# Two graph-attention layers on one core: the memsets between the row gathers are taken out

## The chip, the core and the metric

The kernel runs on one core of a Trainium2 chip. The metric is the time of one execution in microseconds (us) on the device; lower is better. Three runs of the kernel before gave 4551.79, 4556.36 and 4559.20 us, so its median is 4556.36 us.

## The reference

The inputs are 6250 nodes with 256 features each, 200000 edges (source `src`, destination `dst`, sorted by destination) and 32 features for each edge. The nodes are normalised and cut at zero, and two graph-attention layers follow, the first with four heads of 64 features, the second with one head of 256. What one layer does is this (`x` is the node table, `n` the number of nodes):

```
te = relu(edge_attr @ We + be) * exp(x @ Wo + bo)[src][:, None]
s2, d2, ea2 = _add_self_loops(src, dst, te, n)
hx = (x @ Wg).reshape(n, h, f)
he = (ea2 @ Wge).reshape(-1, h, f)
al = leaky_relu(einsum(hx, a_s)[s2] + einsum(hx, a_d)[d2] + einsum(he, a_e), 0.2)
m  = segment_max(al, d2);  al = exp(al - m[d2])
al = al / segment_sum(al, d2)[d2]
out = segment_sum(hx[s2] * al[:, :, None], d2) + b
```

A self loop is added for every node, whose edge features are the mean over the node's incoming edges. Layer 0 ends with `relu(out + x)`; layer 1 adds its input, the input of layer 0 and the raw node features. So for every edge the row of its source node has to be fetched (`hx[s2]`), weighted with a softmax over the edges of one destination, and summed per destination.

## The kernel before, in words

The 200000 edges are cut into chunks of 128 (`P`), and 24 chunks (`C`) make a superchunk. A layer has 66 superchunks (`NS`): 64 of 24 chunks, then one of 14 and one of 13, 1563 chunks in all. One step of the main loop is one superchunk of one layer, so there are 132 steps; `k` counts them, and a step's superchunk within its layer is `s`.

**Prologue** (`prologue`, L203 and on). The node features are loaded, normalised and multiplied with the layer-0 weights; the resulting rows (features, attention terms, the exponential gate) are stored as a table `T[0]` in device memory. During this time GpSimd (POOL) also fetches the raw feature rows of step 0's edges with 24 indirect DMAs of its own (`first_rows`, L249); no other POOL instruction stands between two of these, apart from three places where normalisation statistics are worked out.

**Gather** (`gather`, L792 to L803). For each step, POOL issues one indirect DMA for each chunk: 128 rows of the layer's table (268 floats in layer 0, one of a row pair in layer 1) go to the 128 partitions of one slot of a tile `G` in SBUF (24 slots of 270 floats). There are three `G` tiles, used in turn (`self.gp[st["k"] % 3]`), so the gather of step `k` may start when step `k-3` has done its sums. After every indirect DMA of every step but step 0, POOL also writes zeros to a tile `gap` of 128x208 floats, which no other instruction reads:

```
            nc.gpsimd.indirect_dma_start(
                out=G[:, c, 0:L.TW], out_offset=None, in_=self.rows[L.l][0:n * (1 + L.l), :],
                in_offset=bass.IndirectOffsetOnAxis(ap=idx[:, c:c + 1], axis=0))
            if st["k"]:
                nc.gpsimd.memset(self.gap, 0.0)
```

Step 0's rows come from the prologue, so the loop of `gather` issues 1539 + 1563 = 3102 indirect DMAs. Each waits for the landing of the eighth indirect DMA before it (eight semaphores in turn), and a step's first one also for its `G` tile to be free.

**A step** (`edges`, L615 and on, is an order written out by hand; a tile framework sets semaphores, but moves nothing). In the iteration of step `k` the instructions are put out in this order: POOL gets the gather of step `k+1`; VectorE (DVE) takes `logits(k)` (its first instruction, L987, needs all rows of `G(k)`), then prepares step `k+1` (`spread`, `parts`), TensorE (PE) transposes the run maxima of step `k` (`ends`, L1010), PE and ScalarE (ACT) work out the edge features of step `k+1` (`rphase1`, L885 and L890; `rphase2`, L899; `adst`, L959), DVE goes on with `links` and `maxima` of step `k`, multiplies all rows of `G(k)` with their weights (`scale`, L1095), adds what is carried over from the step before (`carried`, L1080 to L1085), and PE sums the rows per destination (`sums`, L1105, for each of 24 chunks a product with a one-hot matrix `S`, which DVE writes at L930; the profile shows each product as two matmuls). Meanwhile DVE turns and reduces what belongs to step `k+1` (`edge_rows`, L973 and on) and finishes the nodes of step `k-1` (`finish`); in layer 0 their rows go through PE again (L1198, L430) and to the table `T[1]` of layer 1 with a DMA issued by SyncE (SP, L1239). ACT moves the sums from PSUM to `U` (`evict`, L1110).

So DVE, PE and ACT work on step `k` and prepare `k+1`, while POOL, which has nothing but gathers (and the memsets) in its queue in the middle of a layer, fetches the rows of step `k+1`. What ties POOL to the others is `G`: L987 waits for the last landing of a step's gather, and a gather waits for its tile.

**End of a layer** (`ending`, L709 and on). The last two steps are interleaved, POOL helps with the nodes there (L1178 to L1192), the last rows of `T[1]` are stored, and only then does the first gather of layer 1 start, since any of its rows may be wanted. At the end of layer 1 the last rows of the result are scattered (L1249).

Of the kernel before, what the change touches and what calls it, by code (L numbers as in the profile page):

```python
# [22 lines left out]
F32 = mybir.dt.float32  # L23
# [8 lines left out]
P = 128  # L32
# [47 lines left out]
class Kernel:  # L80
# [322 lines left out]
    def fixed_rows(self):  # L403
        nc, cp = self.nc, self.cp
        self.crow = cp.tile([1, D + self.L[0].H], F32, name="crow")
        self.cl = [cp.tile([36, P + 1], F32, name=f"cl{i}") for i in range(2)]
        for t in self.cl:
            nc.gpsimd.memset(t, -BIG)

        self.cnt = cp.tile([P, self.NS, 2], F32, name="cnt")  # L410
        self.mt = cp.tile([P, 4 * C + 4], F32, name="mt")
        self.gap = cp.tile([P, 208], F32, name="gap")
        self.fb = [cp.tile([P, 37 * C], F32, name=f"fb{i}") for i in range(2)]
        for t in [self.mt] + self.fb:
            nc.gpsimd.memset(t, 0.0)


        self.aq = [cp.tile([P, 4, 32], BF, name=f"aq{i}") for i in range(2)]
        for t in self.aq:
            nc.gpsimd.memset(t, 0.0)  # L420
        self.trow1 = []
        L1 = self.L[1]
        for i in range(2):
            self.trow1.append(cp.tile([P, 2 * L1.TW], F32, name=f"t1row{i}"))
            nc.gpsimd.memset(self.trow1[i][:, L1.TW + D:], 0.0)
# [366 lines left out]
    def gather(self, st):  # L792
        nc, L = self.nc, st["L"]
        st["G"] = G = self.G0 if st["k"] == 0 else self.gp[st["k"] % 3].tile([P, C, 270], F32, name="G")
        n = self.N
        idx = self.src[:, st["o"]:st["o"] + st["C"]]
        last = st["C"] - 1
        for c in (range(0) if st["k"] == 0 and self.CX > last else (last, *range(last))):
            nc.gpsimd.indirect_dma_start(  # L799
                out=G[:, c, 0:L.TW], out_offset=None, in_=self.rows[L.l][0:n * (1 + L.l), :],  # L800
                in_offset=bass.IndirectOffsetOnAxis(ap=idx[:, c:c + 1], axis=0))
            if st["k"]:
                nc.gpsimd.memset(self.gap, 0.0)  # L803

    def pair(self, k):

# [660 lines left out]
```

## Time and profile before

| What | Value |
|---|---|
| Median of three runs | 4556.36 us |
| Time of the profiled execution | 4555.93 us |
| Its span (first to last instruction) | 4554.1 us |
| POOL busy | 3915.8 us, 86% of the span |
| PE busy / DVE busy / ACT busy | 3065.9 / 2901.8 / 516.8 us |
| Indirect DMAs in `gather` (L799) | 3102 |
| Memsets of `gap` (L803) | 3102 |
| Mean granted TensorE clock | 0.743 |

The profile is one execution taken by the hardware profiler. Times are in us unless marked ns. A line of the table of groups reads: code line, engine, operation, what is written <- what is read, shape, count, then the busy time and the mean ns of one, then the time that the engine was idle just before these instructions and what ended most of that idle time; "issue" means that the engine waited for nothing that the profile shows. A line of the timeline reads: start, duration, engine, code line, operation, and in brackets the idle time before it and what ended it. For an indirect DMA on POOL the duration is the time that POOL itself works on it; when the data has landed is told apart from that ("DMA to landing"). In the table of stretches each engine has its busy time and its number of instructions, then come the granted TensorE clock as a share of full speed, the share of time that the 16 DMA engines were busy, and GB/s. The chain of work that ended last reaches back only 0.38 and 0.71 us in this profile (it ends at a wait of the program's end), so it does not help here.

### The profile page before, as it was taken

What the parts mean: (1) busy time and instruction counts of PE and PEld (TensorE: products, weight loads), DVE (VectorE), ACT (ScalarE), POOL (GpSimd) and SP (SyncE); (2) the same over time, 40 slices, a digit from 0 to 9 for tenths busy, and PEclk for the clock granted to TensorE, in tenths of its full rate; (3) what the DMA queues carried; (4) which work ended last, traced back from release to release, by engine and by line L of the source; (5) the groups of instructions that cost most, each with busy time, mean ns of one, the idle gap of its engine ahead of it and who ended that gap; (6) DMA issues with size and microseconds to landing.
All of it is one profiled execution on the core that took longest, in us unless ns stands there. A gap on an engine that the chain in (4) does not pass through costs nothing. (4 is left out here: it accounts for less than half of the span.)

```text
span 4554.1 us, 37613 instructions
## 1 busy us (share of the span) xinstructions
PE 3065.9 (67%) x9916; PEld 1899.5 (42%) x9916; DVE 2901.8 (64%) x6675; ACT 516.8 (11%) x1150; POOL 3915.8 (86%) x6365
## 2 busy tenths in 40 slices
PE   8777677667677677677746566666666665666665
PEld 6444444444444344444424334333343343433433
DVE  7877667677677677676745555555554555555655
ACT  5111111111111111111100000000000000000000
POOL 6888888888888888888878888888888888888885
PEclk9877777777777777777767777777777777777777
DMA  6444444444444444444434444444444444444442
GB/s 224 130 136 134 126 129 136 124 127 136 125 128 135 125 128 135 125 130 134 119 98 124 116 128 122 118 128 128 111 128 121 124 123 128 122 116 122 128 116 74
DMA packets 231112, 576.39 MB, mean 127 GB/s; under 512 B 63097, under 2 KB 87871, under 8 KB 230825
## 3 DMA queue, kind: packets, MB, share of 16 engines
q0 software_dynamic: 150144, 422.75, 35.2%
q1 hardware_dynamic: 80331, 150.52, 10.0%
q8 instruction: 79, 1.29, 0.1%
q14 instruction: 142, 1.16, 0.1%
q10 hardware_dynamic: 416, 0.67, 0.1%
HBM read 542.72 MB, written 31.09 MB: 126 GB/s over the span
## 5 line engine op out<-in xcount | busy, mean ns | idle before, releaser
L799 POOL DMA_INDIRECT G<-T,src x3102 | 2969.6, 957 | 553.1 <-issue 518.7
L1105 PE MATMUL u<-G,S 128*128 128x270 f32 (+1 forms) x6252 | 1461.0, 393 | 106.7 <-DVE G L1085 97.6
L1105 PEld LDWEIGHTS u<-G,S 128*128 128x128 f32 x6252 | 1189.5, 192 | 388.0 <-DVE G L1085 162.1
L803 POOL MEMSET gap<- 128x208 f32 x3102 | 893.3, 288 | 1.8
L1095 DVE TENSOR_TENSOR G<-G,kps 128x6144 f32<-128x6144 f32 (+3 forms) x136 | 853.0, 6274 | 0.0
L885 PE MATMUL y<-ea,webd 64*128 64x384 f32 (+1 forms) x1056 | 749.7, 860 | 67.3 <-ACT R L890 66.7
L1010 PE MATMUL lf<-ident,fb 128*36 128x128 f32 (+1 forms) x132 | 53.3, 404 | 1093.3 <-DVE fb L1002 772.3
L987 DVE TENSOR_TENSOR G<-rt,G 128x96 f32<-128x96 f32 (+1 forms) x132 | 30.2, 228 | 1138.9 <-DMA G<-T,src 1138.6
L1010 PEld LDWEIGHTS lf<-ident,fb 128*36 128x36 f32 (+1 forms) x132 | 15.7, 119 | 1134.6 <-DVE fb L1002 819.2
L899 PE MATMUL zad<-R,wea 128*64 128x384 f32 (+1 forms) x1056 | 476.0, 815 | 0.5 <-DVE aq L952 0.3
L890 ACT ACTIVATE R<-y,webd 128x768 f32<-128x768 f32 x260 | 233.2, 897 | 2015.2 <-PE lf L1027 1647.7
L930 DVE TENSOR_TENSOR S<-kps,loc 128x3072 f32<-128x3072 f32 x132 | 437.5, 3315 | 4.5
L885 PEld LDWEIGHTS y<-ea,webd 64*128 64x128 f32 x1056 | 300.9, 314 | 311.8 <-issue 192.5
L899 PEld LDWEIGHTS zad<-R,wea 128*64 128x64 f32 x1056 | 160.7, 207 | 319.0 <-issue 214.0
L945 PE MATMUL zad<-a,Q 128*128 128x12 bf16 (+1 forms) x132 | 24.9, 188 | 174.6 <-DVE a L943 174.6
L430 PE MATMUL fin<-wg,h1T 128*128 128x260 f32 x264 | 135.3, 667 | 2.3 <-ACT h1T L1200 2.3
L973 DVE STREAM_TRANSPOSE rt<-zad 128x768 f32<-128x768 f32 (+1 forms) x130 | 124.9, 960 | 12.1 <-PE zad L959 11.2
L914 DVE TENSOR_TENSOR lb<-lb,kps 128x1536 bf16<-128x1536 bf16 (+1 forms) x68 | 112.7, 1658 | 0.0
L1110 ACT ACTIVATE U<-u 128x270 f32<-128x270 f32 (+1 forms) x132 | 51.9, 393 | 493.7 <-PE u L1105 493.7
L1041 DVE SCALAR_TENSOR_TENSOR m<-fpen,lf,m 128x24 f32<-128x24 bf16 (+1 forms) x66 | 16.4, 249 | 132.8 <-PE lf L1027 132.6
L945 PEld LDWEIGHTS <-Q 128*128 128x128 bf16 x132 | 13.7, 104 | 208.3 <-DVE a L943 198.6
L430 PEld LDWEIGHTS fin<-wg,h1T 128*128 128x128 f32 x264 | 75.6, 316 | 52.1 <-issue 36.6
(201 smaller groups left out, 2287.5 us busy)
## 6 DMA issues: line engine op xcount, KB each, us to landing
G<-T,src POOLq DMA_INDIRECT x3102, 2.8
ea<-in_ea_dram SPq DMA_DIRECT2D x64, 768.0 KB
lb<-locrow SPq DMA_DIRECT2D x64, 384.0 KB
T<-t1row SPq DMA_DIRECT2D x66, 227.5 KB
tw<-T SPq DMA_DIRECT2D x66, 225.8 KB
tw<-T SPq DMA_DIRECT2D x66, 117.2 KB
tw<-in_x_dram SPq DMA_DIRECT2D x66, 112.0 KB
out_dram<-fb SPq DMA_DIRECT2D x64, 112.0 KB
```

The lines of the kernel that those rows point to most:

```text
L430: self.nc.tensor.matmul(ps[:, :L.MW], hT[:, k, :], self.wg[L.l][:, k, :], start=(k == 0), stop=(k == 1))
L799: nc.gpsimd.indirect_dma_start(out=G[:, c, 0:L.TW], out_offset=None, in_=self.rows[L.l][0:n * (1 + L.l), :], in_offset=bass.IndirectOffset ...
L803: nc.gpsimd.memset(self.gap, 0.0)
L885: nc.tensor.matmul(y[:, o], self.webd[l][r, :], ea[r, w], start=True, stop=True)
L890: nc.scalar.activation(R[:, i, :32 * c].rearrange("p (b n) -> p b n", b=2), y.rearrange("p (b n) -> p b n", b=2)[:, :, :16 * c], AF.Relu, ...
L899: nc.tensor.matmul(st["zad"][i * PH:(i + 1) * PH, o], self.wea[l][0], R[:, i, w], start=True, stop=False)
L914: V.tensor_tensor(lb[:, :, :n], lb[:, :, :n], self.k_part.unsqueeze(2).to_broadcast([P, i, n]), op=OP.is_equal)
L930: nc.vector.tensor_tensor(st["S"][:, c0:c1, :], self.k_iota.unsqueeze(1).to_broadcast(w), self.loc[:, o + c0:o + c1].unsqueeze(2).to_broad ...
L973: V.transpose(rv[:, :32 * c].rearrange("p (b n) -> p b n", b=2), z.rearrange("p (b n) -> p b n", b=2)[:, :, :16 * c])
L1010: self.nc.tensor.transpose(self.lf[0:e.shape[1], 1:P + 1], e, self.ident)
L1095: nc.vector.tensor_tensor(v, v, pw[:, c0:c1, :].unsqueeze(3) .to_broadcast([P, c1 - c0, H, L.F]), op=OP.mult)
L1105: nc.tensor.matmul(st["u"][:, :L.W], S[:, i, :], G[:, i, 0:L.W], start=(j == 0), stop=(j == c - 1))
```

## The change

The tile `gap` and the memset after every indirect DMA of `gather` go. Nothing else changes: PE, DVE, ACT and SP keep the same instructions in the same order, and POOL keeps its own without the 3102 memsets. The waits of the indirect DMAs stay as they are.

```
         self.mt = cp.tile([P, 4 * C + 4], F32, name="mt")
-        self.gap = cp.tile([P, 208], F32, name="gap")
         self.fb = [cp.tile([P, 37 * C], F32, name=f"fb{i}") for i in range(2)]
...
             nc.gpsimd.indirect_dma_start(
                 out=G[:, c, 0:L.TW], out_offset=None, in_=self.rows[L.l][0:n * (1 + L.l), :],
                 in_offset=bass.IndirectOffsetOnAxis(ap=idx[:, c:c + 1], axis=0))
-            if st["k"]:
-                nc.gpsimd.memset(self.gap, 0.0)
```

More of the change, by code (lines that the diff above doesn't have):

```diff
@@ L411, in fixed_rows @@
         self.mt = cp.tile([P, 4 * C + 4], F32, name="mt")
-        self.gap = cp.tile([P, 208], F32, name="gap")
         self.fb = [cp.tile([P, 37 * C], F32, name=f"fb{i}") for i in range(2)]
@@ L801, in gather @@
                 in_offset=bass.IndirectOffsetOnAxis(ap=idx[:, c:c + 1], axis=0))
-            if st["k"]:
-                nc.gpsimd.memset(self.gap, 0.0)
     def pair(self, k):
```

## The prediction

> **What bounds the kernel now.** I read the page's busy times and groups first, to see what the memsets stand beside.
>
> ```profile
> span 4554.1 us, 37613 instructions
> ...
> PE 3065.9 (67%) x9916; PEld 1899.5 (42%) x9916; DVE 2901.8 (64%) x6675; ACT 516.8 (11%) x1150; POOL 3915.8 (86%) x6365
> ...
> L799 POOL DMA_INDIRECT G<-T,src x3102 | 2969.6, 957 | 553.1 <-issue 518.7
> L803 POOL MEMSET gap<- 128x208 f32 x3102 | 893.3, 288 | 1.8
> ```
>
> POOL is the busiest engine, and its idle time before gathers is nearly all "issue": it waits for nobody. Gathers, memsets and issue gaps make 2969.6 + 893.3 + 553.1 = 4416 of 4554 us. Whether the others wait for POOL is in the waits, over layer 0 in its steady part (57 steps) and over layer 1 (64 steps):
>
> ```profile
> DVE G L987 <- DMA G<-T,src: 353.4, 57, 7.6
> ...
> DVE G L987 <- DMA G<-T,src: 770.4, 64, 24.3
> ...
> 1520.63 0.26 DVE L987 TENSOR_TENSOR G<-rt,G 128x96 f32<-128x96 f32 x1 [4.66 <-DMA G<-T,src]
> ```
>
> DVE waits for gathered rows in every step: 353.4 / 57 = 6.2 us a step in layer 0, 770.4 / 64 = 12.0 in layer 1. The third row, from the timeline, is the step with the shortest wait that I found in layer 0 after its first few: 4.66 us. So in the middle of both layers the steps run at the pace of POOL, with that much room below it. The pace itself, by stretches (from the first gather of step 6 to the last of step 63, then from layer 1's first to the last of its 64th step; L799 alone, then L803 alone):
>
> ```profile
> 264.30:2230.10 1965.80, 1334.77 (x1392) 0.74 0.47 129
> 2309.75:4474.80 2165.05, 1468.15 (x1536) 0.73 0.45 122
> ...
> 264.30:2230.10 1965.80, 400.84 (x1392) 0.74 0.47 129
> 2309.75:4474.80 2165.05, 441.82 (x1535) 0.73 0.45 122
> ```
>
> One gather takes 1965.80 / 1392 = 1.412 us in layer 0 (33.9 us a step) and 2165.05 / 1536 = 1.410 in layer 1: 0.959 and 0.956 of DMA instruction, 0.288 of memset, and 0.165 left between memset and next gather.
>
> **The change part by part.** One thing goes: 3102 memsets. What POOL does between two gathers changes with them, and this decides the size:
>
> ```profile
> 1517.79 0.95 POOL L799 DMA_INDIRECT G<-T,src  x1 [0.17 <-issue]
> 1518.74 0.29 POOL L803 MEMSET gap<- 128x208 f32 x1
> 1519.19 0.95 POOL L799 DMA_INDIRECT G<-T,src  x1 [0.17 <-issue]
> ...
> 7.12 1.19 POOL L249 DMA_INDIRECT G<-in_x_dram,src  x1 [0.31 <-issue]
> ...
> 12.41 0.95 POOL L249 DMA_INDIRECT G<-in_x_dram,src  x1 [0.30 <-issue]
> 13.66 0.95 POOL L249 DMA_INDIRECT G<-in_x_dram,src  x1 [0.30 <-issue]
> ...
> 21.17 0.95 POOL L249 DMA_INDIRECT G<-in_x_dram,src  x1 [0.30 <-issue]
> ```
>
> Now a memset starts at the gather's end, and the next gather 0.17 us after it. The prologue's gathers (L249) stand directly behind one another, as all will after the change, and there the gap is 0.30 us, so part of the memset is covered by an issue time that comes back: from 12.41 to 21.17 are seven gathers, 1.251 us each. A gather would thus take 0.959 + 0.302 = 1.261 us and save 0.288 + 0.165 - 0.302 = 0.151 us, not 0.288. The gap's bounds: 0.17 (a gather behind other POOL work) below; above, 0.31 together with the longest gather near it, 1.19, which is 1.50 us a gather, more than now. I take 0.302, from the rows that have the very same sequence, these eight without a break; they fetch rows of 256 floats against 268, and the DMA instruction takes 0.95 in both.
>
> *Layer 0.* 24 x 0.151 = 3.6 us a step come off the gathers. The shortest wait of 4.66 us covers that, so every steady step should get shorter by it, to 24 x 1.261 = 30.3 us, and DVE should still wait, 6.2 - 3.6 = 2.6 us on the average. In the first steps this doesn't hold:
>
> ```profile
> 162.62 0.95 POOL L799 DMA_INDIRECT G<-T,src  x1 [5.81 <-ACT U L1110]
> ...
> 184.24 0.26 DVE L987 TENSOR_TENSOR G<-rt,G 128x96 f32<-128x96 f32 x1
> 209.77 0.26 DVE L987 TENSOR_TENSOR G<-rt,G 128x96 f32<-128x96 f32 x1
> ```
>
> DVE does not wait there; POOL, ahead, waits at 162.62 for its tile (until ACT has moved step 0's sums). From there on the gathers run without a stop to 2230.1: 61 steps or 1464 gathers, which would end at 162.6 + 1464 x 1.261 = 2008.7, so 221 us earlier. The steps begin to wait some steps later than now (around the ninth), but what they wait for then is this same row of gathers.
>
> *Between the layers* nothing is won: the last steps and the rows of the second table, from 2230.1 to layer 1's first gather, are a chain of DVE, PE and DMAs.
>
> ```profile
> 2309.75 1.06 POOL L799 DMA_INDIRECT G<-T,src  x1 [10.18 <-DMA T<-t1row]
> ...
> 4476.98 0.20 DVE L987 TENSOR_TENSOR G<-rt,G 128x24 f32<-128x24 f32 x1 [13.00 <-DMA G<-T,src]
> 4496.32 0.24 DVE L987 TENSOR_TENSOR G<-rt,G 128x14 f32<-128x14 f32 x1 [0.40 <-DMA G<-T,src]
> 4514.86 0.18 DVE L987 TENSOR_TENSOR G<-rt,G 128x13 f32<-128x13 f32 x1 [3.06 <-DMA G<-T,src]
> ```
>
> *Layer 1.* 1536 gathers x 0.151 = 232 us, with waits of 12 us above them. The 27 gathers of the last two steps have little to give: the waits left there are 0.40 and 3.06 us, so 3 us more.
>
> Sum: 221 + 232 + 3 = 456 us. The profiled execution took 4555.9 us (span and 1.8), the median is 4556.4, half a microsecond from it: 4556 - 456 = 4100 us. What is queued behind the memsets is only the next gather, no wait is added, and no other queue changes. What faster gathers trigger is denser DMA traffic: the share of 0.47 in the stretch above becomes 0.47 x 1.412 / 1.261 = 0.53, far from full.
>
> Two covers must hold. One is the landing: each gather waits for the eighth before it, now 8 x 1.412 = 11.3 us earlier, then 8 x 1.261 = 10.1.
>
> ```profile
> DMA to landing us min/median/max: 2.7/2.8/8.2
> ...
> DMA to landing us min/median/max: 2.7/5.8/6.8
> ```
>
> The first row is L799's, the second L249's, from the crowded prologue. Both maxima lie below 10.1: no cost. The other is the TensorE clock, which falls to half when PE rests and has come back before the sums:
>
> ```profile
> 986.00:988.00 2.00, 2.00 (x4) 1.17 (x4) 1.81 (x3) 0.16 (x1) 1.67 (x4) 0.50 0.29 77
> 996.00:998.00 2.00, 2.00 (x11) 1.65 (x10) 2.00 (x1) 0.00 (x0) 1.68 (x3) 1.00 0.73 203
> ...
> 1029.58 11.21 PE L1105 MATMUL u<-G,S 128*128 128x270 f32 x48 [0.50 <-DVE G L1085]
> ...
> 173.35 13.96 PE L1105 MATMUL u<-G,S 128*128 128x270 f32 x48 [3.25 <-DVE G L1085]
> ```
>
> At 986 us the clock is 0.50 under the edge features, at 996 it is 1.00 under the sums, which take 11.21 us. In the early, unwaiting steps one set of sums took 13.96 us behind a rest of 3.25, so a step can lose 2.75 us by a poor phase; the room of 2.6 us about covers it. [...]
>
> **The rivals.**
>
> *The gathers get slower without a pause* (slower than before). Place: the DMA instruction on POOL itself. From 1.412 - 0.302 = 1.110 us a gather on, the gain is gone. For it: the 1.19 at 7.12. Against: the next rows at 0.95. If all took the 1.19 + 0.31 = 1.50, the time would be 4556 + 3000 x 0.09 = 4826 us.
>
> *The sums lose the clock* (slower too). At half clock they take 2 x 11.21 = 22.4 us. PE's round is then the bound:
>
> ```profile
> 1013.92 0.40 PE L1010 MATMUL lf<-ident,fb 128*36 128x128 f32 x1 [8.51 <-DVE fb L1002]
> ...
> 4444.26 0.42 PE L1010 MATMUL lf<-ident,fb 128*33 128x128 f32 x1 [8.60 <-DVE a L940]
> ...
> 4456.57 10.83 PE L1105 MATMUL u<-G,S 128*128 128x261 f32 x48 [0.33 <-DVE G L1085]
> ```
>
> From L1010 to the start of the sums are 15.7 us in layer 0 and 12.3 in layer 1; with sums of 22.4 and 21.7 a round takes 38.1 and 34.0. That gives 4556 + 61 x 4.2 + 64 x 0.2 = 4825. It costs layer 0 something from about two thirds of this loss on. Against it: from 157 to 266 us, where the steps follow one another with almost no wait, the clock was 0.86, higher than later.
>
> ```profile
> 157.00:266.00 109.00, 91.05 (x318) 59.05 (x316) 96.33 (x227) 16.91 (x39) 91.09 (x147) 0.86 0.45 126
> ```
>
> *Layer 0 turns to its own chain.* If its steps don't get shorter (late loads, or the lost clock in part), only layer 1 gains: 4556 - 235 = 4321 us; in part, between 4190 and that.
>
> *The gap shrinks to 0.17.* A gather takes 0.959 + 0.165 = 1.124, a step 27.0, less than layer 0's chain of 33.9 - 6.2 = 27.7. Layer 0 would gain 61 x 6.2 = 378, layer 1 1536 x 0.286 = 439: 3739 us. Only gathers behind other POOL work show that gap.
>
> **How the numbers follow.** Forecast as worked out (3990 to 4190): 0.66. Layer 0 on its own chain (4190 to 4450): 0.10. The short gap (3739 to 3990): 0.05. Slower gathers 0.10 and lost clock 0.07, together 0.17. No change, if the memset stood for something that takes its place to the nanosecond: 0.02. The range of 3739 to 4450 leaves out 0.19. Faster by more than 0.2% (9 us, about what a measurement can tell here): 0.81; within: 0.02; slower: 0.17.
>
> **What would show it.** Right: L799 with about 0.957 us a gather and 0.30 us before it ("issue", some 930 us in all), steady stretches of 30.3 us a step, L987's wait down to 2 to 3 us in layer 0 and 8 to 9 in layer 1, clock not below 0.74. Wrong: L799 well over 1.0 us, or its idle time ended by "DMA G<-T,src" (landing), or sums of 20 us at a clock near 0.5, or L987 without wait in layer 0.

## The result, and the profile after

The changed kernel takes 4091.98 us (median of 5 runs, 4090.76 to 4095.94) against 4556.36 us before (median of 5 runs, 4551.79 to 4559.20). The ratio is 0.8984, with a 95% interval of 0.8975 to 0.8994: 464 us less. The forecast was 4100 us, a gain of 456.

The page of the changed kernel, busy times and the group of the gathers (L798 is the former L799, L984 the former L987, L1102 the former L1105):

```profile
span 4088.9 us, 34512 instructions
...
PE 3041.5 (74%) x9916; PEld 1889.4 (46%) x9916; DVE 2882.0 (70%) x6675; ACT 516.2 (13%) x1150; POOL 3015.5 (74%) x3263
...
L798 POOL DMA_INDIRECT G<-T,src x3102 | 2955.9, 953 | 984.9 <-issue 916.3
```

POOL lost 900 us of busy time, but its idle time before gathers rose from 553 to 985 us, nearly all of it still "issue". So the removed 893 us of memsets did not come back whole: 984.9 - 553.1 = 432 us of them had stood over an issue time that has to be paid anyway. The timeline of POOL shows it:

```profile
1001.27 0.95 POOL L798 DMA_INDIRECT G<-T,src  x1 [0.30 <-issue]
1002.53 0.95 POOL L798 DMA_INDIRECT G<-T,src  x1 [0.30 <-issue]
```

The pace of the gathers, over the same steps as in the prediction (from the first gather of step 6 to the last of step 63, then from layer 1's first to the last of its 64th step; L798 alone):

```profile
252.16:2007.61 1755.45, 1331.74 (x1392) 0.77 0.53 145
2086.88:4012.22 1925.34, 1457.76 (x1536) 0.76 0.51 138
```

One gather takes 1755.45 / 1392 = 1.261 us in layer 0 and 1925.34 / 1536 = 1.253 in layer 1, a step 30.3 and 30.1 us. DVE's waits for rows, in layer 0's steady part and in layer 1:

```profile
DVE G L984 <- DMA G<-T,src: 162.1, 55, 5.0
...
DVE G L984 <- DMA G<-T,src: 540.4, 64, 20.7
```

They shrank from 6.2 to 2.9 us a step and from 12.0 to 8.4 (540.4 / 64), and they are still there in nearly every step: POOL is still what the steps wait for, with less room behind it. What stands below the gathers in layer 0 is already near. The waits of single steps differ; three of steps 9 to 12:

```profile
375.19 0.26 DVE L984 TENSOR_TENSOR G<-rt,G 128x96 f32<-128x96 f32 x1 [0.60 <-DMA G<-T,src]
406.89 0.26 DVE L984 TENSOR_TENSOR G<-rt,G 128x96 f32<-128x96 f32 x1 [3.37 <-DMA G<-T,src]
...
467.46 0.26 DVE L984 TENSOR_TENSOR G<-rt,G 128x96 f32<-128x96 f32 x1 [4.57 <-DMA G<-T,src]
```

The whole gain, by the two profiles' spans (4554.1 - 4088.9 = 465 us): up to the last gather of step 63, 2230.1 - 2007.6 = 222.5 us; from there to layer 1's first gather 79.7 us before and 79.3 after, so 0.4 us; over layer 1's 1536 gathers 2165.05 - 1925.34 = 239.7; the remaining 2 to 3 us in the last two steps.

### The profile page after: what moved, and what is told of

Its sections match the earlier page's. It is cut to its first block, busy times and chain, and to the rows that moved or that the text cites. A ratio compares the mean times of both kernels' runs of the same rounds, so it can differ in the third digit from the quotient of the medians.

```text
span 4088.9 us, 34512 instructions
## 1 busy us (share of the span) xinstructions
PE 3041.5 (74%) x9916; PEld 1889.4 (46%) x9916; DVE 2882.0 (70%) x6675; ACT 516.2 (13%) x1150; POOL 3015.5 (74%) x3263
## 5 line engine op out<-in xcount | busy, mean ns | idle before, releaser
L798 POOL DMA_INDIRECT G<-T,src x3102 | 2955.9, 953 | 984.9 <-issue 916.3
L1102 PE MATMUL u<-G,S 128*128 128x270 f32 (+1 forms) x6252 | 1453.9, 392 | 105.9 <-DVE G L1082 97.1
L1102 PEld LDWEIGHTS u<-G,S 128*128 128x128 f32 x6252 | 1184.5, 191 | 383.8 <-DVE G L1082 160.5
L882 PE MATMUL y<-ea,webd 64*128 64x384 f32 (+1 forms) x1056 | 739.3, 850 | 67.4 <-ACT R L887 66.8
L984 DVE TENSOR_TENSOR G<-rt,G 128x96 f32<-128x96 f32 (+1 forms) x132 | 30.3, 230 | 708.2 <-DMA G<-T,src 707.4
L1041 DVE TENSOR_TENSOR mt<-fpen,lf 128x96 f32<-128x96 bf16 (+1 forms) x66 | 16.7, 253 | 118.3 <-PE lf L1024 118.1
```

Source lines behind the costliest of these rows:

```text
L798: nc.gpsimd.indirect_dma_start(out=G[:, c, 0:L.TW], out_offset=None, in_=self.rows[L.l][0:n * (1 + L.l), :], in_offset=bass.IndirectOffset ...
L882: nc.tensor.matmul(y[:, o], self.webd[l][r, :], ea[r, w], start=True, stop=True)
L1102: nc.tensor.matmul(st["u"][:, :L.W], S[:, i, :], G[:, i, 0:L.W], start=(j == 0), stop=(j == c - 1))
```

## The experiments

The theory after the result: in the middle of both layers a step is as long as POOL's round of 24 gathers, and a round is the DMA instruction (0.95 us), what stands between two gathers on POOL, and an issue time; beneath it lie the steps' own chains. The rivals: that the gain belongs to one layer only, that the memsets cost by their length alone, that the steps' own chains change when they don't pause.

### One column in place of 208

```
-                nc.gpsimd.memset(self.gap, 0.0)
+                nc.gpsimd.memset(self.gap[:, 0:1], 0.0)
```

> The memset after each gather stays, but writes one column (128x1, about 0.09 us by the small memsets of the prologue) in place of 208. Theory (a memset starts at the gather's end, the next gather 0.17 us after the memset; only a gather directly behind a gather pays 0.30): a gather takes 0.955 + 0.09 + 0.17 = 1.215 us, less than the 1.256 without memsets, so 3000 x 0.04 = 120 us below the changed kernel: about 3970 us. Rival (a gather needs its 0.30 us of issue after the gather before it, whatever stands between): never below the changed kernel, 4090 us or, if the memset adds to it, up to 4360.

Measured: 4106.38 us (4104.24 to 4107.14), ratio to before 0.9014 (0.8999 to 0.9029). That is not below the changed kernel but 14 us above it: here the rival of that expectation was right. Groups and timeline of POOL:

```profile
L799 POOL DMA_INDIRECT G<-T,src x3102 | 2957.0, 953 | 644.6 <-issue 593.2 <-ACT h L309 17.9 <-ACT U L1110 14.3
L803 POOL MEMSET gap<- 128x1 f32 x3102 | 367.3, 118 | 0.7
```

```profile
1002.71 0.12 POOL L803 MEMSET gap<- 128x1 f32 x1
1003.02 0.95 POOL L799 DMA_INDIRECT G<-T,src  x1 [0.19 <-issue]
1003.97 0.11 POOL L803 MEMSET gap<- 128x1 f32 x1
...
1017.96 0.12 POOL L803 MEMSET gap<- 128x1 f32 x1
1018.61 0.94 POOL L799 DMA_INDIRECT G<-T,src  x1 [0.53 <-issue]
```

A memset of 0.118 us, then 0.19 us of issue instead of the 0.17 behind the long memset: from the end of a gather to the start of the next 0.305 us pass (median), the same as without any memset. 3102 instructions more on the engine that sets the pace cost 14 us in all, and hardly any of it is in the ordinary gap. In the full steps of both layers every 106th gap (28 of them; the last row above ends one) is 0.49 us or longer, most of them 0.65, and what these have beyond 0.305 us sums to 12 us. The kernel before has longer gaps at the same 28 gathers; the changed kernel has none (its longest is 0.311). What POOL does in them, no view shows.

### Without memsets in layer 0 alone

```
-            if st["k"]:
+            if L.l:
                 nc.gpsimd.memset(self.gap, 0.0)
```

> The memsets go in layer 0 alone and stay as they were in layer 1. Theory (each layer gains by its own gathers): 4556 - 221 = 4335 us, half of the whole gain, and L987 waits 2.9 us a step in layer 0 and 11.8 in layer 1. Rival (the gain is made in layer 1, where the waits are long, and layer 0 mostly turns to its own chain): near 4500 us or more.

Measured: 4332.82 us (4331.49 to 4335.77), ratio 0.9513 (0.9497 to 0.9529): 223 us of the gain, where 221 were expected. The waits for rows, in layer 0's steady part and in layer 1:

```profile
DVE G L987 <- DMA G<-T,src: 166.5, 57, 5.0
...
DVE G L987 <- DMA G<-T,src: 745.8, 63, 16.4
```

2.9 us a step in layer 0, as in the changed kernel, and 11.8 in layer 1, as in the kernel before. Each layer gains by its own gathers. The 241 us that are left belong to layer 1.

### Two memsets

```
                 nc.gpsimd.memset(self.gap, 0.0)
+                nc.gpsimd.memset(self.gap, 0.0)
```

> Two memsets of 128x208 after each gather. Theory (POOL's round of gather, memset and issue is the step): one memset more costs 0.288 us a gather without any further issue gap, 1.70 us a gather, so 4556 + 3000 x 0.288 = 5420 us. Rival (part of it is covered by other waits): less than 5300 us.

Measured in one execution: 5595.65 us, 1041 us above before, more than either side had expected. Groups of POOL:

```profile
L799 POOL DMA_INDIRECT G<-T,src x3102 | 2955.0, 953 | 592.3 <-issue 563.9 <-ACT h L309 18.2 <-DMA T<-t1row 10.2
L803 POOL MEMSET gap<- 128x208 f32 x3102 | 896.3, 289 | 0.7
L804 POOL MEMSET gap<- 128x208 f32 x3102 | 841.8, 271 | 178.3
```

The second memset costs its own 0.271 us and 178.3 / 3102 = 0.057 us of idle time before it, which the expectation had put at nothing (it waits for a semaphore that the memset before it sets; both write `gap`). That is 841.8 + 178.3 = 1020 us over 3102 gathers, 0.33 us each, against 1041 measured; the idle time before gathers is 39 us longer than before, the gathers themselves 15 us shorter. So what is added between two gathers, once they are more than 0.30 us apart, comes out in the total about in full.

### Fewer gathers

This edit is to the changed kernel; the rows of 11 of 24 chunks are left out, so it computes something else.

```
-        for c in (range(0) if st["k"] == 0 and self.CX > last else (last, *range(last))):
+        few = st["k"] > 3 and last == C - 1
+        if few:
+            nc.gpsimd.memset(G[:, 1:last:2, :], 0.0)
+        for c in (range(0) if st["k"] == 0 and self.CX > last else
+                  (last, *range(0, last, 2)) if few else (last, *range(last))):
```

> From step 4 on, only 13 of the 24 chunks of a full superchunk are fetched; the other 11 slots of G are set to zero by one memset of about 2.8 us, so most of the neighbours' rows are left out of the result. POOL's round becomes 13 x 1.256 + 3 = 19 us. Theory (behind the gathers stand the steps' own chains, 27.3 us in layer 0 and 21.9 in layer 1 by period less wait): 4092 - 61 x 2.85 - 62 x 8.2 = about 3410 us, L987 without wait in both layers. Rival (the chains themselves get shorter or longer when they don't pause, for instance by the TensorE clock): layer 0 steps of 25 us or of 30 us and more, 3250 or 3600 us.

Measured in one execution: 3445.81 us. Steps of layer 0 (the two rows are steps 7 and 63) and of layer 1 (steps 68 and 128), in the timeline of DVE:

```profile
322.99 0.26 DVE L988 TENSOR_TENSOR G<-rt,G 128x96 f32<-128x96 f32 x1
...
1892.52 0.26 DVE L988 TENSOR_TENSOR G<-rt,G 128x96 f32<-128x96 f32 x1 [0.23 <-issue]
...
2032.21 0.20 DVE L988 TENSOR_TENSOR G<-rt,G 128x24 f32<-128x24 f32 x1
...
3343.86 0.20 DVE L988 TENSOR_TENSOR G<-rt,G 128x24 f32<-128x24 f32 x1
```

With POOL's round well below them, the steps take (1892.52 - 322.99) / 56 = 28.0 us in layer 0 and (3343.86 - 2032.21) / 60 = 21.9 in layer 1, with next to no wait for rows. Layer 1 is as expected; layer 0 is 0.7 us a step longer than period less wait had told (27.3), and that makes up the 36 us by which 3410 was too low. The trace shows DVE instructions that got longer beside the memset of `G`, which this experiment adds. The first two rows are of this run, the third of the changed kernel (L937 there is L941 here):

```profile
465.16 2.57 POOL L799 MEMSET G<- 128x2970 f32 x1 [9.44 <-issue]
465.62 2.14 DVE L941 CAST a<-tw 128x4 bf16<-128x4 f32 x1
...
378.99 0.17 DVE L937 CAST a<-tw 128x4 bf16<-128x4 f32 x1
```

Between steps 8 and 63 this cast took more than 0.4 us in 25 of 55 steps, and L589 (it writes `lpen`, in 0.21 us otherwise) 2.66 us in 8, each time while the memset ran. These long instructions make DVE 1.0 us a step busier there than in the changed kernel; in layer 1, whose step came out as expected, DVE is not busier. That the 0.7 us come from the memset is thus likely, though not tested by a run of its own, and 28.0 us is better read as an upper bound for the chain of layer 0. Read so, the changed kernel's 30.3 us has at least 2.3 us of room in layer 0 and 8 us in layer 1 before something else than the gathers takes over; before, it was at least 5.9, and 12.

### A still smaller memset, and half of one

```
-                nc.gpsimd.memset(self.gap, 0.0)
+                nc.gpsimd.memset(self.gap[0:32, 0:1], 0.0)
```

> The memset after each gather writes one column of 32 partitions, the shortest memset of the prologue (91 ns there, against 118 ns for 128x1 in the run before). Theory now (a floor: from a gather's end to the next gather pass at least 0.30 us, and a memset's time plus some 0.17 us where that is more): the same as the changed kernel, 4090 to 4107 us, with an idle time of about 0.21 us between memset and gather. Rival (memset plus a fixed 0.19 us, which at 118 ns came near 0.30 by chance): 0.28 us in place of 0.305, so 3000 x 0.025 = 75 us less, about 4025 us.

Measured: 4104.87 us (4104.02 to 4106.82), ratio 0.9011 (0.8996 to 0.9026). By its time it does not tell the two apart, because its premise failed: the memset takes 118 ns here too, not 91.

```profile
L803 POOL MEMSET gap<- 32x1 f32 x3102 | 365.6, 118 | 0.8
```

The other one has `self.gap[:, 0:104]` in the same place.

> The memset after each gather writes 104 columns, half of before's 208; between 118 ns for one column and 288 ns for 208 lie about 0.20 us. Theory (floor, or memset plus 0.167 us): 0.953 + 0.20 + 0.167 = 1.32 us a gather, 0.065 more than the changed kernel, so about 4290 us. Rival (the pace between 4092 and 4556 follows the memset's length from zero on, without a floor): half of the columns, half of the difference, about 4330 us and more.

Measured in one execution: 4299.48 us, where the theory said 4290 and the rival 4330 or more.

```profile
L799 POOL DMA_INDIRECT G<-T,src x3102 | 2973.8, 959 | 560.1 <-issue 520.9 <-ACT h L309 17.9 <-DMA T<-t1row 10.2
L803 POOL MEMSET gap<- 128x104 f32 x3102 | 623.4, 201 | 1.5
```

```profile
1001.66 0.21 POOL L803 MEMSET gap<- 128x104 f32 x1
1002.04 0.95 POOL L799 DMA_INDIRECT G<-T,src  x1 [0.17 <-issue]
```

Side by side; the fourth column is the median time from the end of one gather to the start of the next ("between gathers"):

| Memset between | its mean time, us | issue after it | between gathers, us | time of the kernel, us |
|---|---|---|---|---|
| none | 0 | 0.30 | 0.305 | 4091.98 |
| 32x1 | 0.118 | 0.19 | 0.305 | 4104.87 |
| 128x1 | 0.118 | 0.19 | 0.305 | 4106.38 |
| 128x104 | 0.201 | 0.17 | 0.364 | 4299.48 |
| 128x208 (before) | 0.288 | 0.17 | 0.451 | 4556.36 |

The time between gathers does not fall below 0.30 us, and for the two long memsets it is the memset's time and 0.17. That 0.118 and 0.19 make 0.30 could still be a coincidence of a short memset and a fixed time after it. The run with 32x1 settles this by itself, for not all of its memsets took 0.118 us:

```profile
1004.95 0.95 POOL L799 DMA_INDIRECT G<-T,src  x1 [0.19 <-issue]
1005.88 0.17 POOL L803 MEMSET gap<- 32x1 f32 x1
1006.20 0.95 POOL L799 DMA_INDIRECT G<-T,src  x1
```

Here the memset took 0.17 us, and the next gather started 0.15 us after it, again 0.30 us after the gather before. In the two runs with one column 116 memsets took between 0.13 and 0.18 us; the idle time after them shrank to as little as 0.13 us, and the median time between gathers stayed 0.305. So there is no fixed time after a memset, and behind these short ones a floor of 0.30 us holds. How the floor passes into the memset's time and 0.17, the runs do not show: 0.18 and 0.17 would already be 0.35.

## Why the prediction was right

*The bound.* It said that POOL's gathers set the pace in the middle of both layers, from the waits of DVE. The run with two memsets (slower by about what POOL's round grew) and the one with 13 gathers a step (646 us faster than the changed kernel) show it from both sides. The waits that are left came out as forecast, 2.9 us a step in layer 0 (2 to 3) and 8.4 in layer 1 (8 to 9), and so did the DMA share of 0.53.

*The price of the one edit.* The step that decided the size was to take not the memset's 0.288 us off a gather, but 0.288 + 0.165 - 0.302 = 0.151, because gathers directly behind one another had shown 0.30 us of issue in the prologue. Had the memset been priced by its group alone, the forecast would have been 4556 - 3000 x 0.288 = 3692 us, 400 too low. Measured were 1.412 - 1.261 = 0.151 us in layer 0, and 1.410 - 1.253 = 0.156 in layer 1.

*The sum.* Layer 0 221 us forecast, 222.5 measured in the profiles, 223 with the memsets gone in layer 0 alone. Between the layers nothing, measured 0.4. Layer 1 232 forecast, 239.7 measured: this is the mis-sized term, and most of the 8 us by which 4100 was too high. The gathers there take 1457.76 / 1536 = 0.949 us each without memsets against 0.956 with them, 10 us over 1536; the forecast had kept 0.956. The gap came out at 1.253 - 0.949 = 0.304 us, not 0.302, which takes some 4 us of it back. The median DMA instruction of a gather went from 0.952 to 0.946 us in both layers; in layer 0 more single ones are longer than 0.98 us (136 of 1392 against 81), so that the mean hardly moved there (0.959 to 0.957). Why, no run shows; that layer 0 came out so close owes something to this. The end: 3 us forecast, 2 to 3 measured.

*The first steps.* The waits for rows start later than before, as was said (by the timeline of DVE in step 8, with 4.89 us, where it was 3.02 us in step 5), and the row of gathers from step 3 on is what counts.

*The rivals.* The gathers did not get slower without a pause: 953 ns on the average, against 957. Their landing is the same and its longest, 8.2 us, is below the 10.1 us of eight gathers, so the wait for the eighth gather before costs nothing:

```profile
DMA to landing us min/median/max: 2.7/2.8/8.2
```

The sums did not lose the clock; it rose from 0.743 to 0.771 on the average, and layer 0's sums stayed at 11.21 us in nearly all steps. Three sets of sums of the changed kernel, and one of the kernel before:

```profile
1026.68 11.21 PE L1102 MATMUL u<-G,S 128*128 128x270 f32 x48 [1.20 <-DVE G L1082]
1058.18 11.43 PE L1102 MATMUL u<-G,S 128*128 128x270 f32 x48 [0.33 <-DVE G L1082]
1087.58 11.21 PE L1102 MATMUL u<-G,S 128*128 128x270 f32 x48 [0.86 <-DVE G L1082]
...
622.38 13.04 PE L1105 MATMUL u<-G,S 128*128 128x270 f32 x48 [0.40 <-DVE G L1085]
```

The loss of 2.75 us that the prediction read from one set of sums of 13.96 us stayed in the first steps: the changed kernel has a set of 14.20 us in step 1, with the granted clock at 0.50 from 172 to 178 us, but in steps 8 to 62 none longer than 11.43 us. The kernel before has four of 13.0 us there; all four began at a granted clock of 0.50 (the one at 622.38 until 626 us, with 1.00 from 627 us on), while the set of the changed kernel at 1026.68 ran at 1.00 from its start. What decides when the clock comes back, no run shows. Layer 0 did not turn to its own chain: this lies at 28.0 us or less, at least 2.3 below the gathers. And the gap did not shrink to 0.17: it is 0.30 us behind another gather, and a short memset put in between does not make it shorter (the runs with one column).

## What to carry to other kernels

Price an instruction that is taken out of an engine's stream by the time from the end of the instruction before it to the start of the one after it, with and without it; look for a place in the same trace where the two neighbours already stand directly together. Here two thirds of what the memsets and the gaps behind them took (0.30 of 0.45 us) was a time that passes before the next indirect DMA in any case. And before trusting a gain on the bound engine, read the shortest wait of the others in the steady steps: it gives a cautious figure for how much of the gain can be had before the next bound takes over (4.66 us here, where the run with fewer gathers showed at least 5.9).

## What the runs showed of the hardware

Between two indirect DMAs on POOL at least 0.30 us passed in these runs, and a memset of 0.12 to 0.18 us fitted into them almost for nothing: 3102 memsets of one column cost 14 us together, 12 of them in 28 longer gaps. A memset on POOL took 0.118 us there for 1 column of 128 partitions and for 1 column of 32 alike, and two memsets of the same tile had 0.057 us of idle time between them. With 104 and 208 columns a memset took 0.201 and 0.288 us. While a POOL memset of 128x2970 ran for 2.57 us, two small DVE instructions beside it (L941 and L589) took 2.14 and 2.66 us in place of 0.17 and 0.21.
